# A graph-network kernel on four full engines: the adjacency is copied into the score bank by ScalarE, and the linear row is added by the instruction that takes the extreme

## The chip, the cores and the metric

The kernel runs on one core of a Trainium2 chip. The metric is the device time of one execution in microseconds: the kernel before takes 4812.59 us (median of three runs, 4811.78 to 4815.49).

## What is computed

The input `x` has 64 graphs of 256 nodes with 128 features; `adj` is one 256 x 256 adjacency for all. Everything is fp32. Four residual layers follow each other, each on `h = relu(layernorm(x))`:

- layer 0: five steps of a gated recurrence (`adj @ h`, two gates, a tanh candidate);
- layer 1: Chebyshev hops with `adj`, a linear map, relu;
- layer 2: `adj @ h + h`, a linear map, rows divided by their norm;
- layer 3: pairwise attention, in the reference

```python
pre = s1[:, :, None, :] + s2[:, None, :, :] + b_lin
h = jnp.where(pre >= 0, pre, ALPHA * pre)
e = jnp.einsum('bije,e->bij', h, a) + bias
attn = jax.nn.softmax(e, axis=2)
out = jax.nn.sigmoid(jnp.einsum('bij,bjf->bif', attn, x))
```

In the first line `s1` and `s2` are `h` times the two halves of `adj` (it stands in the place of `W`). For each of 64 graphs layer 3 needs 256 x 256 node pairs with 256 features each: this is where the time goes. In the end the 256 x 256 scores `e` of a graph are the sum of three things: a nonlinear part, for each pair of nodes and each feature; the adjacency; and a part linear in `s2`, one row of 256 numbers per graph ("the linear row"; what is linear in `s1` falls out of the softmax).

## The kernel before

**Tiles and scores.** The graphs go in 32 pairs. A pair's query nodes are cut into 64 slots of four nodes for each of both graphs (2048 slots in all; 32 slots are a *unit*, that is 128 query nodes of both graphs). A slot has two tiles `rl` of 128 x 4 x 2 x 256 numbers (features by query nodes by graphs by the other nodes), the minimum or the relu of what `s1` and `s2` give: kind 0 (first half of the features) and kind 1 (second half). `work_on_tile` (L933 on) makes them: VectorE kind 0 in one instruction (L953), ScalarE kind 1 in eight (L961), GpSimd either kind in eight (L967). TensorE's `score` sums a tile over its features with a window of signs and adds the result into the unit's bank of the accumulator memory (PSUM), in eight matmul instructions (L1041).

**Joined slots.** In a share of the slots, `SHARE = (4, 13)`, GpSimd makes the second tile in a form of its own (kind 2), and a transfer that GpSimd issues adds it to the slot's kind 0 tile in memory (`add_pair`, L987). Such a slot is scored once, not twice. The last 96 slots have none. There are 14 tile buffers.

**A unit's bank.** Each unit's scores accumulate in a bank of 128 x 512 (two graphs by 256). `bank_ready` (L997) and `fill_bank` (L1004) fill it before the first score: one VectorE instruction (L1006) writes adjacency rows plus the linear row `lin`. The first pair's two units ("alone": its graphs are treated one by one) instead get the adjacency by matmuls in `score`. `tail` (L827) follows the unit's last score. VectorE adds an odd feature's step (L839, two instructions of 128 x 256: minimum of `s2o` and `s1o`, plus the bank, into `sc`), takes the maximum of the rows, negated (L844); ScalarE takes exponentials with it as bias (L848); then come a turn on TensorE (L447), a copy (L856), the product with `h3`, and `o` (L876), which SyncE sends out. For the first two units the tail also adds `lin`.

**The other work.** `front` brings a pair through layers 0 to 2 and makes the operands of layer 3. Its steps are small instructions on all engines; `norm` (L475) goes from VectorE (statistics) over GpSimd (inverse roots) to ScalarE. `lin` and `s2o` come through small transfers by way of main memory into the tile `rows`.

**What sets the order.** The program is written out in one order per engine by a planner (the loop at the end of the function). `ran(engine, us, ...)` (L106) advances a clock of planned durations, such as `TURN`, `STATS`, `ELEMENTS`; whichever engine's clock is least takes the next thing that is ready. Tails come first, then fronts, then fills, added pairs or scores, then new tiles. So tiles are shared out by the planned durations, not on the chip: there each engine runs its list in order and waits on semaphores.

Of the kernel before, what the change touches and what calls it, by code (L numbers as in the profile page):

```python
# [8 lines left out]
F32 = mybir.dt.float32  # L9
AF = mybir.ActivationFunctionType  # L10
OP = mybir.AluOpType
AX = mybir.AxisListType
PSUM = bass.MemoryType.PSUM

P = 128
NB = 2
# [5 lines left out]
MOST_POSITIVE = -MOST_NEGATIVE  # L22
PE, DVE, ACT, POOL = ENGINES = (mybir.EngineType.PE, mybir.EngineType.DVE, mybir.EngineType.Activation, mybir.EngineType.Pool)
SLOTS = 64
SHARE = (4, 13)
AHEAD_OF = 2
ALONE = 96
LOW = 1
# [4 lines left out]
def kernel(  # L33
# [50 lines left out]
    nc = tc.nc  # L84
    B, N, D = x.shape
# [20 lines left out]
    def ran(engine, us, *after):  # L106
        start = max(clock[engine], 0.0, *after)
        clock[engine] = start + us
        return clock[engine] + SEEN[engine]
# [10 lines left out]
    def of_spare(bank):  # L120

        return [b for b in spare if bank < 2 or id(b[0]) in WRITTEN]
# [14 lines left out]
    def by_feature(b, nb=NB):  # L137
        return b[:, 0:nb * N].rearrange("p (b n) -> p b n", b=nb)
# [320 lines left out]
    def feat(name, **kw):  # L459
        return work.tile([P, NB, N], F32, name=name, **kw)  # L460
# [7 lines left out]
    SHORT = dict(tag="short", bufs=12)  # L468


    PROJECT, MIX, TURN, PRODUCT, PRODUCTS = (None, 0.44, 0.86), (None, 0.88, 1.74), (None, 0.38, 0.60), (None, 0.45, 0.88), (None, 1.33, 2.64)
    COPY, BIASED, TANH, ELEMENTS = (None, 0.32, 0.48), (None, 0.40, 0.58), (None, 0.40, 0.57), (None, 0.36, 0.61)
    NORMED, STATS, LAST = (None, 0.78, 1.55), (None, 0.50, 0.87), (None, 0.55, 1.04)

    def norm(src, since, h):  # L475

        nb = src.shape[1]
        stats = work.tile([P, nb * NC, 3], F32, name="stats", bufs=4)
        mv = work.tile([P, nb * NC, 2], F32, name="mv", bufs=4)
        s, h = rows_of(src), rows_of(h)[:, :, 0:D]  # L480
        yield DVE, since
        for k in range(0, nb * NC, 2):
            nc.vector.bn_stats(stats[:, k:k + 2, :].rearrange("p k s -> p (k s)"), s[:, k:k + 2, :].rearrange("p k d -> p d k"))
        nc.vector.tensor_reduce(mv[:, :, 0], stats[:, :, 1:2], AX.X, OP.add, negate=True)
        t = ran(DVE, STATS[nb], since) + 0.1
        yield POOL, t
        inverse_root(mv[:, :, 1], stats[:, :, 2], 1.0 / D, OP.mult, LN_EPS, OP.add)
        nc.gpsimd.tensor_mul(mv[:, :, 0], mv[:, :, 0], mv[:, :, 1])  # L488
        t = ran(POOL, 1.69, t)
        yield ACT, t  # L490
        for k in range(nb * NC):
            nc.scalar.activation(h[:, k, :], s[:, k, :], AF.Relu, bias=mv[:, k, 0:1], scale=mv[:, k, 1:2])  # L492
        return ran(ACT, NORMED[nb], t)

    READY = {}
# [327 lines left out]
    def across(u):  # L823

        return [(0, c) if READY[u]["alone"] else (c, u[1]) for c in range(NB)]

    def tail(u, pe, since):  # L827

        ops = READY[u]
        x3, h3, pe = ops["x3"], ops["h3"], [by_feature(pe[0])[:, k, :] for k in range(NB)]  # L830
        yield DVE, max(since, ops["t_lin"])
        used = banks_of.pop(u)[0]
        if ops["alone"]:
            nc.vector.tensor_add(by_feature(used), by_feature(used), ops["lin"].to_broadcast([P, NB, N]))
            since = ran(DVE, ELEMENTS[2], since, ops["t_lin"])
            yield DVE, since
        sc = feat("sc", **SHORT)
        for k, (b, c) in enumerate(across(u)):
            nc.vector.scalar_tensor_tensor(sc[:, k, :], ops["s2o"][:, b, :], ops["s1o"][:, b, c:c + 1], pe[k], op0=OP.min, op1=OP.add)  # L839
        t = ran(DVE, 0.8, since)  # L840
        spare.append([used, t])
        yield DVE, t
        nmx = work.tile([P, NB], F32, name="nmx")
        nc.vector.tensor_reduce(nmx, sc, AX.X, OP.max, negate=True)  # L844
        t = ran(DVE, ELEMENTS[2], t)
        yield ACT, t
        for b in range(NB):
            nc.scalar.activation(sc[:, b, :], sc[:, b, :], AF.Exp, bias=nmx[:, b:b + 1], scale=1.0)  # L848
        t_s = ran(ACT, 0.8, t)
        yield PE, t_s, 1  # L850
        b = take()
        to_token(b[0], sc)
        t = ran(PE, TURN[2], t_s, b[1])
        yield ACT, t
        wT = tok("wT", **SHORT)
        nc.scalar.copy(wT, by_token(b[0]))  # L856
        t = ran(ACT, COPY[2], t)
        spare.append([b[0], t])
        yield PE, t, 1
        bank = take()  # L860
        po = bank[0][:, :NB * (D + 1)].rearrange("p (b d) -> p b d", b=NB)
        for k, (b, _) in enumerate(across(u)):
            for c in range(NC):
                side_by_side(po[:, k, :], wT[:, k, c, :], h3[:, b, c, :], c == 0, c == NC - 1)
        t = ran(PE, PRODUCT[2], t, bank[1])
        yield DVE, t
        rs = work.tile([P, NB], F32, name="rs")
        nc.vector.reciprocal(rs, po[:, :, D])
        t = t_s = ran(DVE, 0.15, t)
        yield ACT, t  # L870
        for k in range(NB):
            nc.scalar.activation(po[:, k, 0:D], po[:, k, 0:D], AF.Tanh, scale=rs[:, k:k + 1])
        t = ran(ACT, 0.9, t, t_s)
        yield DVE, t
        o = work.tile([P, NB, D], F32, name="o")
        nc.vector.scalar_tensor_tensor(o, po[:, :, 0:D], 0.5, x3[:, 0] if ops["alone"] else x3[:, :, u[1], :], op0=OP.mult, op1=OP.add)  # L876
        t = ran(DVE, 0.36, t)
        spare.append([bank[0], t])
        p, k = u
        nc.sync.dma_start(out[p * NB + k].rearrange("(c p) d -> p c d", p=P) if ops["alone"] else  # L880
                          out[p * NB:(p + 1) * NB, k * P:(k + 1) * P, :].rearrange("b p d -> p b d"), o)
        TAILED.add(u)
# [8 lines left out]
    banks_of = {}  # L891
# [105 lines left out]
    def bank_ready():  # L997

        u = next((u for u in UNITS if u not in left and u not in banks_of), None)
        if u not in READY or READY[u]["alone"] or len(banks_of) == 2 or all(where(slot(k))[0] < u for k in range(3)):  # L1000
            return None
        return (max(READY[u]["t_lin"], min(b[1] for b in of_spare(2))), u) if of_spare(2) else None

    def fill_bank(u):  # L1004
        bank, free = take(2)
        nc.vector.tensor_add(by_feature(bank), adj_n[:, u[1]:u[1] + 1, :].to_broadcast([P, NB, N]), READY[u]["lin"])  # L1006
        banks_of[u] = bank, ran(DVE, ELEMENTS[2], free, READY[u]["t_lin"])

    def score_ready():

# [85 lines left out]
    while scored[0] < 2 * NSLOT or CHAINS:  # L1096
        while begun_fronts[0] < NPAIR and begun_fronts[0] < 2 + (scored[0] + 2 * SLOTS - 1) // (2 * SLOTS):
            begin_front()
        e = min(now, key=now.get)
        todo = []  # L1100
        for key in CHAINS:
            since = chain_ready(key, e)
            if since is not None:
                todo.append((since, (0, key) if isinstance(key, tuple) else (1, key), key))
        if e == PE:
            best = score_ready()
            if best:
                todo.append((best[0], (2,), best[1]))
        else:
            since = tile_ready(e)  # L1110
            if since is not None:
                todo.append((since, (3,), None))
            if e == DVE and bank_ready():
                todo.append((bank_ready()[0], (2,), bank_ready()[1]))
            pair = pair_ready()
            if e == POOL and pair and e not in begun:
                todo.append((pair[0] + SLACK, (2,), pair[1]))
        ready = [x for x in todo if x[0] <= now[e] + 0.05]
        if ready:
            if e == PE and len(tiles) <= LOW:  # L1120
                ready = [x for x in ready if x[1] == (2,)] or ready
            _, (rank, *_), what = min(ready, key=lambda x: x[1])
            if rank < 2:
                advance(what)
            elif e == PE:
                score(what)
            elif e == DVE and rank == 2:
                fill_bank(what)
            elif rank == 2:
                add_pair(what)  # L1130
            else:
                work_on_tile(e)
            in_order()
            now[e] = max(now[e], clock[e])
        else:
            later = [x[0] for x in todo] + [t for t in now.values() if t > now[e]]
            now[e] = min(later) if later else now[e] + 1.0
# [31 lines left out]
```

## Time and profile before

| | |
|---|---|
| runs: median (lowest to highest) | 4812.59 us (4811.78 to 4815.49) |
| the profiled execution: its time, its span | 4794.9 us, 4793.1 us |
| mean granted TensorE clock | 0.997 |
| accumulating transfers (`rl<-rl`) | 600 of 1 MB, 8.1 us from issue to landing |
| that queue's packets | 65.5% of 16 transfer engines' span |
| VectorE tiles (L953) | 1743 |
| ScalarE tile instructions (L961) | 10104 |
| GpSimd tile instructions (L967) | 6280 and 2440 |
| scoring matmuls (L1041) | 17864 and 10104 |

Busy time of an engine is the union of its instructions' records. In a group of instructions the mean is that of single records, which overlap at their ends, so a start-to-start distance can be shorter than the mean. "Idle before" says what an engine waited for. The chain that ended last is followed back from the last instruction, each step to what released it. Names: `bank` is a PSUM bank, `rl` a tile, `rows` the tile that holds `lin` and `s2o`; PE is TensorE, PEld its weight loads, DVE VectorE, ACT ScalarE, POOL GpSimd, SP SyncE.

### The profile page before, as it was taken

How to read it: one execution, taken by the hardware profiler on the slowest of the kernel's cores; microseconds unless marked ns; L12 is line 12 of the kernel's file. 1: busy time of each engine (PE TensorE's matmuls, PEld its weight loads, DVE VectorE, ACT ScalarE, POOL GpSimd, SP SyncE). 2: the span in 40 equal slices, each digit the busy share in tenths (PEclk: the TensorE clock that was granted, in tenths of full speed). 3: DMA queues.
4: the chain of work that ended last, by engine and by line, in shares of the span. 5: the costliest groups of instructions: out<-in, count | busy, mean ns of one | idle time of the engine just before them, and what ended most of it. 6: DMA issues, size and time to landing. Idle time of an engine off the chain costs nothing.

```text
span 4793.1 us, 132928 instructions
## 1 busy us (share of the span) xinstructions
PE 4718.4 (98%) x51591; PEld 1740.7 (36%) x51591; DVE 4647.5 (97%) x3502; ACT 4659.3 (97%) x12220; POOL 4619.2 (96%) x9823
## 2 busy tenths in 40 slices
PE   9999999999999999999999999999999999999999
PEld 4333333333333333333333333333333333333333
DVE  5999999999999999999999999999999999999998
ACT  5999999999999999999999999999999999999999
POOL 2999999999999999999999999999999999999998
PEclk9999999999999999999999999999999999999999
DMA  0777777777777777777777777777767776777730
GB/s 23 157 143 152 146 152 150 144 149 154 152 143 154 146 146 157 147 151 145 150 146 155 149 148 147 149 151 154 148 139 153 155 150 142 145 151 148 147 69 5
DMA packets 131523, 672.70 MB, mean 140 GB/s; under 512 B 14920, under 2 KB 50120, under 8 KB 54088
## 3 DMA queue, kind: packets, MB, share of 16 engines
q0 software_dynamic: 86400, 629.18, 65.5%
q1 hardware_dynamic: 43768, 35.01, 2.5%
q8 instruction: 403, 6.60, 0.5%
q14 instruction: 232, 1.90, 0.1%
q10 hardware_dynamic: 720, 0.00, 0.0%
HBM read 26.48 MB, written 8.52 MB: 7 GB/s over the span
## 4 chain that ended last, share of the span: by engine, by line
PE 47%; DVE 15%; POOL 11%; ACT 8%; DMA 4%; issue 4%; POOLq 0%; DVEq 0%; ACTq 0%
PE bank L1041 31%; PE bank L414 14%; DVE rl L953 11%; POOL rl L967 9%; ACT rl L961 6%; DMA rl<-rl 4%; PE bank L447 1%; POOL rl L987 1%; DVE bank L1006 1%; ACT h L492 1%; PE bank L439 0%; DVE bank L626 0%; POOL mv L409 0%; DVE hT L630 0%; DVE d L622 0%
## 5 line engine op out<-in xcount | busy, mean ns | idle before, releaser
L961 ACT ACTIVATE rl<-bank,s1b 128x256 f32<-128x256 f32 x10104 | 4072.5, 833 | 10.1 <-DMA rl<-rl 6.5
L953 DVE TENSOR_TENSOR rl<-s1a,bank 128x2048 f32<-128x2048 f32 x1743 | 3894.9, 2277 | 26.1 <-DMA rl<-rl 13.1
L967 POOL TENSOR_SCALAR rl<-s2n,s1b 128x256 f32<-128x256 f32 x6280 | 3033.4, 829 | 13.9 <-DMA rl<-rl 3.1
L1041 PE MATMUL bank<-rl,win_n 128*32 128x512 f32 x17864 | 2226.3, 594 | 19.9 <-DMA rl<-rl 13.4
L1041 PE MATMUL bank<-rl,win 128*32 128x512 f32 x10104 | 1349.9, 594 | 0.0
L967 POOL TENSOR_SCALAR rl<-s2c,s1a 128x256 f32<-128x256 f32 x2440 | 1190.6, 783 | 5.2 <-PE bank L1041 1.4
L1041 PEld LDWEIGHTS bank<-rl,win_n 128*32 128x32 f32 x17864 | 583.5, 110 | 1181.0 <-issue 964.9
L987 POOL DMA_DIRECT2D rl<-rl x600 | 651.7, 1105 | 9.4 <-issue 4.8
L1041 PEld LDWEIGHTS bank<-rl,win 128*32 128x32 f32 x10104 | 335.1, 110 | 675.6 <-issue 529.4
L414 PE MATMUL bank<-mT,wts 128*32 128x512 f32 x2480 | 325.6, 595 | 4.5 <-DVE rh L587 4.5
L414 PE MATMUL bank<-adj_t,h 128*32 128x256 f32 x4960 | 297.8, 380 | 5.1 <-ACT h L641 5.0
L414 PEld LDWEIGHTS bank<-adj_t,h 128*32 128x32 f32 x4960 | 157.7, 110 | 165.8 <-ACT h L641 40.8
L492 ACT ACTIVATE h<-x,mv 128x128 f32<-128x128 f32 x376 | 170.4, 654 | 22.7 <-POOL mv L488 22.4
L583 ACT ACTIVATE bank<-bank,gate_b 128x512 f32<-128x512 f32 (+1 forms) x165 | 158.3, 959 | 17.1 <-PE bank L414 15.3
L414 PE MATMUL bank<-mT,w 128*32 128x512 f32 x1240 | 163.2, 596 | 0.0
L414 PE MATMUL bank<-rh,u5t 128*32 128x512 f32 x1240 | 162.7, 595 | 0.0
L414 PE MATMUL bank<-hT,wts 128*32 128x512 f32 x1240 | 162.1, 593 | 0.0
L539 ACT COPY mT<-bank 128x512 f32<-128x512 f32 x155 | 145.3, 937 | 16.0 <-PE bank L414 15.9
L606 ACT ACTIVATE bank<-bank,gate_b 128x512 f32<-128x512 f32 (+1 forms) x165 | 153.7, 931 | 6.1 <-PE bank L414 5.8
L619 ACT ACTIVATE bank<-bank,gate_b 128x512 f32<-128x512 f32 x155 | 147.2, 950 | 5.3 <-PE bank L414 5.2
L414 PEld LDWEIGHTS bank<-mT,wts 128*32 128x32 f32 x2480 | 81.0, 110 | 191.8 <-issue 132.5
L409 POOL TENSOR_TENSOR mv<-mv,minus_half 128x4 f32<-128x4 f32 (+1 forms) x132 | 134.2, 1017 | 11.0
(207 smaller groups left out, 3252.7 us busy)
## 6 DMA issues: line engine op xcount, KB each, us to landing
rl<-rl POOLq DMA_DIRECT2D x600, 1024.0 KB, 8.1
rows<-row SPq DMA_DIRECT2D x31, 512.0 KB
xin<-in_x_dram SPq DMA_DIRECT2D x64, 128.0 KB
out_dram<-o SPq DMA_DIRECT2D x64, 128.0 KB
row<-quarter SPq DMA_DIRECT2D x62, 2.0 KB
rows<-row SPq DMA_DIRECT2D x2, 256.0 KB
w_raw<-in_L_gnn_w_w_dram SPq DMA_DIRECT2D x3, 128.0 KB
rl<-in_L_gnn_Theta_dram SPq DMA_DIRECT2D x1, 320.0 KB
```

Of the source, the lines that this page charges most:

```text
L409: nc.gpsimd.tensor_tensor(t, t, minus_half[:, 0:t.shape[1]], op=OP.pow)
L414: nc.tensor.matmul(o[g:g + 32], w[:, g:g + 32], t, start=start, stop=stop, skip_group_check=True)
L492: nc.scalar.activation(h[:, k, :], s[:, k, :], AF.Relu, bias=mv[:, k, 0:1], scale=mv[:, k, 1:2])
L539: nc.scalar.copy(c, seen(bank))
L583: nc.scalar.activation(seen(r), seen(pr), AF.Tanh, bias=br, scale=0.5)
L606: nc.scalar.activation(seen(pr), seen(pr), AF.Tanh, bias=bz, scale=0.5)
L619: nc.scalar.activation(seen(pv), seen(pv), AF.Tanh, bias=bh_n, scale=-1.0)
L953: nc.vector.tensor_tensor(t, rows.to_broadcast(whole), ops["s2a"].unsqueeze(1).to_broadcast(whole), op=OP.min)
L961: nc.scalar.activation(t[:, g, b, :], other(ops["s2b"], b), AF.Relu, bias=rows[:, g, b], scale=-1.0)
L967: nc.gpsimd.tensor_scalar(t[:, part, b, :], other(ops["s2n" if k else "s2c"], b), rows[:, part, b], MOST_NEGATIVE, op0=OP.min, op1=OP.max)
L987: nc.gpsimd.dma_start(out=t.rearrange("p g b n -> p (g b n)"), in_=z.rearrange("p g b n -> p (g b n)"), accum_op=OP.add)
L1041: nc.tensor.matmul(pe[g * 32:(g + 1) * 32, :], w[:, 31 - r:63 - r], flat(t[:, g]), start=False, stop=(left[u] == 0), skip_group_check=True)
```

## The change

The share of joined slots becomes (1, 3). The bank is filled by ScalarE, with the adjacency alone, and the fill no longer depends on `lin`. In the tail the odd feature's step comes first and writes the bank in place; then two `tensor_tensor_reduce` instructions add `lin`, multiply by -1, write `sc`, and give the row's minimum as an accumulated output, so that the reduction apart goes and the exponential gets scale -1. The first two units go the same way, without an add of their own. In the planner `TURN` rises by 0.1 and the time from statistics to GpSimd by 0.4.

```diff
-SHARE = (4, 13)
+SHARE = (1, 3)
...
-    PROJECT, MIX, TURN, PRODUCT, PRODUCTS = (None, 0.44, 0.86), (None, 0.88, 1.74), (None, 0.38, 0.60), (None, 0.45, 0.88), (None, 1.33, 2.64)
+    PROJECT, MIX, TURN, PRODUCT, PRODUCTS = (None, 0.44, 0.86), (None, 0.88, 1.74), (None, 0.48, 0.70), (None, 0.45, 0.88), (None, 1.33, 2.64)
...
-        t = ran(DVE, STATS[nb], since) + 0.1
+        t = ran(DVE, STATS[nb], since) + 0.5
...
-        used = banks_of.pop(u)[0]
-        if ops["alone"]:
-            nc.vector.tensor_add(by_feature(used), by_feature(used), ops["lin"].to_broadcast([P, NB, N]))
-            since = ran(DVE, ELEMENTS[2], since, ops["t_lin"])
-            yield DVE, since
+        used, lin = banks_of.pop(u)[0], ops["lin"]
+        for k, (b, c) in enumerate(across(u)):
+            nc.vector.scalar_tensor_tensor(pe[k], ops["s2o"][:, b, :], ops["s1o"][:, b, c:c + 1], pe[k], op0=OP.min, op1=OP.add)
+        t = ran(DVE, 0.9, since, ops["t_lin"])
+        yield DVE, t
         sc = feat("sc", **SHORT)
+        nmx = work.tile([P, NB], F32, name="nmx")
         for k, (b, c) in enumerate(across(u)):
-            nc.vector.scalar_tensor_tensor(sc[:, k, :], ops["s2o"][:, b, :], ops["s1o"][:, b, c:c + 1], pe[k], op0=OP.min, op1=OP.add)
-        t = ran(DVE, 0.8, since)
+            nc.vector.tensor_tensor_reduce(sc[:, k, :], pe[k], lin[:, b, :], scale=-1.0, scalar=MOST_POSITIVE,
+                                           op0=OP.add, op1=OP.min, accum_out=nmx[:, k:k + 1])
+        t = ran(DVE, 0.8, t)
         spare.append([used, t])
-        yield DVE, t
-        nmx = work.tile([P, NB], F32, name="nmx")
-        nc.vector.tensor_reduce(nmx, sc, AX.X, OP.max, negate=True)
-        t = ran(DVE, ELEMENTS[2], t)
         yield ACT, t
         for b in range(NB):
-            nc.scalar.activation(sc[:, b, :], sc[:, b, :], AF.Exp, bias=nmx[:, b:b + 1], scale=1.0)
+            nc.scalar.activation(sc[:, b, :], sc[:, b, :], AF.Exp, bias=nmx[:, b:b + 1], scale=-1.0)
...
-        return (max(READY[u]["t_lin"], min(b[1] for b in of_spare(2))), u) if of_spare(2) else None
+        return (min(b[1] for b in of_spare(2)), u) if of_spare(2) else None
...
-        nc.vector.tensor_add(by_feature(bank), adj_n[:, u[1]:u[1] + 1, :].to_broadcast([P, NB, N]), READY[u]["lin"])
-        banks_of[u] = bank, ran(DVE, ELEMENTS[2], free, READY[u]["t_lin"])
+        nc.scalar.copy(by_feature(bank), adj_n[:, u[1]:u[1] + 1, :].to_broadcast([P, NB, N]))
+        banks_of[u] = bank, ran(ACT, 0.51, free)
...
-            if e == DVE and bank_ready():
+            if e == ACT and bank_ready():
...
-            elif e == DVE and rank == 2:
+            elif e == ACT and rank == 2:
                 fill_bank(what)
```

## The prediction

> **What bounds the kernel now.** I read the page's busy shares first, then the chain that ended last, then the groups that the diff touches, then the timeline around single fills.
>
> The busy shares (engine, busy us, share of the span, instructions):
>
> ```profile
> PE 4718.4 (98%) x51591; PEld 1740.7 (36%) x51591; DVE 4647.5 (97%) x3502; ACT 4659.3 (97%) x12220; POOL 4619.2 (96%) x9823
> ```
>
> Four engines are full at once. VectorE, ScalarE and GpSimd make the 4096 tiles between them, TensorE scores them, and a third to a half of the makers' missing time lies in the first 100 us (VectorE is busy for 48 of them, ScalarE 46, GpSimd 11 by the windows). So no engine is *the* bound: work taken from one maker is worth only its share of all makers' speed, because the planner shares the tiles out anew. That share is a choice of mine, checked against the chain (shares of the span by line, whole execution):
>
> ```profile
> by line: PE bank L1041 31.1%; PE bank L414 14.1%; DVE rl L953 11.4%; POOL rl L967 8.9%; ACT rl L961 5.9%; DMA rl<-rl 4.5%; issue 3.6%; PE bank L447 1.5%; POOL rl L987 1.1%; DVE bank L1006 0.7%; ACT h L492 0.7%; PE bank L439 0.5%; DVE bank L
> ```
>
> It wanders over all of them. Two entries matter: "DMA rl<-rl", the accumulating transfers, 4.5% or 216 us; and L1006, the bank fill, 0.7% or 34 us, much for 62 instructions. Its group, with the neighbours that I use as prices (count, then busy us, mean ns of one):
>
> ```profile
> L953 DVE TENSOR_TENSOR rl<-s1a,bank 128x2048 f32<-128x2048 f32 x1743 | 3894.9, 2277 | 26.1 <-DMA rl<-rl 13.1 <-POOL rl L967 5.8 <-PE bank L1041 4.6
> L1006 DVE TENSOR_TENSOR bank<-adj_n,rows 128x512 f32<-128x512 f32 x62 | 85.7, 1382 | 0.0
> L839 DVE SCALAR_TENSOR_TENSOR sc<-rows,s1o,bank 128x256 f32<-128x256 f32 x128 | 55.4, 474 | 7.6 <-PE bank L1041 7.6
> L844 DVE TENSOR_REDUCE nmx<-sc 128x2 f32<-128x512 f32 x64 | 43.3, 676 | 0.0
> L876 DVE SCALAR_TENSOR_TENSOR o<-bank,x 128x256 f32<-128x256 f32 x64 | 26.9, 420 | 7.1 <-ACT bank L872 6.9
> L868 DVE RECIPROCAL rs<-bank 128x2 f32<-128x2 f32 x64 | 10.6, 165 | 13.8 <-PE bank L414 12.5 <-ACT rl L961 1.2
> ```
>
> A fill has 512 columns like L844, yet means 1382 ns against 676. One of the twelve over 1.9 us, with GpSimd beside it (start, duration):
>
> ```profile
> 4064.07 0.68 DVE L622 TENSOR_TENSOR d<-bank,hT 128x512 f32<-128x512 f32 x1
> 4064.67 4.92 DVE L1006 TENSOR_TENSOR bank<-adj_n,rows 128x512 f32<-128x512 f32 x1
> 4069.51 0.69 DVE L626 SCALAR_TENSOR_TENSOR bank<-bank,d 128x512 f32<-128x512 f32 x1
> ```
> ```profile
> 4062.30 8.40 POOL L967 TENSOR_SCALAR rl<-s2n,s1b 128x256 f32<-128x256 f32 x16
> ```
>
> The fill has no idle before it; it lasts 4.92 us while GpSimd runs its tile through, and the front step L626 stands behind it. GpSimd loses too: over the trace, its runs of 8 tile instructions beside a fill average 4.53 us (30 runs), the others 3.95 (456); runs of 16, 8.13 and 7.44. That is 0.6 to 0.7 us for a fill.
>
> **The price of a microsecond on each maker.** A tile costs VectorE 3894.9/1743 = 2.235 us, ScalarE 8 x 4072.5/10104 = 3.22, GpSimd 8 x (3033.4+1190.6)/8720 = 3.88. The rates 0.447, 0.310 and 0.258 make 1.016 tiles a us, so a us taken from VectorE is worth 0.44 us of the span, from ScalarE 0.31, from GpSimd 0.25. It holds while GpSimd can exchange tiles with both others: of its 1090 tiles 600 are joined ones, and with 650 some 440 stay free.
>
> **VectorE, removed.** 62 fills: start to start they average 1.32 us, 62 x 1.32 = 82. 64 reductions L844, start to start 0.60: 38. The two first units' adds: 1. Together 121 us.
>
> **VectorE, added.** 128 tensor_tensor_reduce of 128x256, one operand in PSUM, one in SBUF, with an accumulated output; the trace has none. The two L839 instructions stay, only written into the bank (L626 writes a bank and takes what L630 takes into SBUF). The nearest row for the main part is L876, the same operands without a per-partition scalar: 420 ns, where the next starts 0.34 after it. By the row alone, 128 x 0.34 = 44 us. [...] Net -121 + 58 = -63 us (ends -77 and -22), worth -28 (-34 to -10).
>
> Would the new instruction stall like the fill? [...] The trace agrees: L1006 (adj_n and rows both in SBUF) spreads from 677 to 5343 ns, L839 (rows in SBUF, the bank in PSUM) only from 462 to 481. The new pair is bank and row, like L839. [...]
>
> **ScalarE.** 62 copies of adjacency rows into a bank. The like row is L668, a broadcast copy into a bank of the same 128x512; the next starts 0.51 after it. 62 x 0.51 = 32 us, worth +10 (ends 0.47, as the other copies, and 0.55: +9 to +10). Behind a fill in ScalarE's queue stand tiles and front copies; L668 and L700 have no idle before them, so I add no wait. The fill no longer waits for the linear row's transfers. That saves nothing, L1006 having no idle; the row is now first needed at the tail, half a pair later. ACTIVATE stays, with another sign of scale.
>
> **GpSimd and the transfers.** JOINED has 1952 x 4/13 = 600 slots (the page has 600 adds) and will have 650. 50 more issues, each 0.63 us before the next instruction: 31 us. Without fills GpSimd gets 62 x 0.6 = 37 back. Net -6, worth -1 (without the relief +8). Tiles made stay 4096. Each add moves 1 MB: the queue's 65.5% of the transfer engines becomes 71%.
>
> **TensorE.** 50 scores fewer. A score is eight matmul instructions; the chain has 64 of them in 6.87 us, so 0.86 us a score, 43 us in all. I don't add this to the sum: the makers remain, and 43 is more than they give. The bank is held one VectorE step longer in the tail; of 8 banks that is 64 times some 2 us, which I put at nothing (at most +3).
>
> **Planned durations.** TURN +0.1 and the statistics' +0.5 change only the order. GpSimd waits 16.1 us for statistics outside the first long waits, worth at most -4; ScalarE waits 11.6 for turned banks, at most -4. Above: 320 turns planned 0.1 us longer leave TensorE 32 us which the plan thinks used; at its 31% of the chain, +10. I take 0.
>
> [...]
>
> **Sum.** -28 + 10 - 1 = **-19 us**. The profiled execution took 4794.9 (span 4793.1); the runs' median is 4812.6, 17.7 above it, and I carry the difference over: 4775 and **4793**.
>
> Check by the chain, line by line: L1006 -34; scoring 1491 x 50/3496 = -21; transfers 216 x 50/600 = +18; issues 53 x 50/600 = +4; VectorE's tail (+20, of which the chain holds L839's 13%) +3; ScalarE (7% of its tiles are on the chain) +2; GpSimd -4. That is -32. As another path takes over when one is cut, it is the larger end.
>
> **Rivals.** *The stalls did more than their length* (0.17): a 5 us stall delays the front step behind it and all four orders; the chain's -32 is had in full, 4781. For it: L1006's 34 us of chain. Against: three quarters of the fills take under 1 us.
>
> *Nothing comes of it* (0.20): the reduction costs 0.77 (-10 + 10 - 1 = -1) or the new plan's order loses what is saved; 4803 to 4822, about 4812. For it: no row has this instruction. It begins to slow the kernel above 0.77 us.
>
> *Adds land late* (0.23, the slower side): of the 19.9 us that the L1041 matmuls with win_n stand idle, 13.4 are waits for rl<-rl, and landing takes 8.1 us at the median, up to 15.2, while the queue's work is 0.655 x 4793/600 = 5.2. The plan reckons 6.6. Each of the 650 also keeps two of 14 tiles until it lands. If the chain's transfer part grows not by 18 but by 50 us (23%), the chain's gain is gone; at 65, some 4828. For it: the chain's 216 us. Against: waits of all engines for rl<-rl sum to about 82 us, many of them weight loads' that cost little.
>
> **How the numbers follow.** The forecast has 0.40, its own range 4785 to 4802. 0.2% of 4812.6 is 9.6 us, about what measuring this kernel can tell from no change. Faster 0.40 + 0.17 = 0.57, same 0.20, slower 0.23. The range goes from 4766 (the full chain with the reduction's low end) to 4832.
>
> **What the next profile would show.** Right: no VectorE instruction of 128x512 with two SBUF operands, none over 0.8 us but tiles; ACT copies x62 near 0.5 us apart; 128 reductions of 0.34 to 0.55 us start to start; 650 adds, 3446 scores; runs of 8 on GpSimd all near 3.95; VectorE more tiles than 1743, by about 20. Wrong: reductions above 0.77, or a "DMA rl<-rl" share of the chain far above 5% with larger waits of TensorE for it.

## The result, and the profile after

The kernel after takes 4799.74 us (median of nine runs, 4797.11 to 4801.11), the kernel before beside it 4812.59 (4810.66 to 4819.12). The ratio is 0.997, 95% interval 0.9961 to 0.9979: 12.9 us faster, where 19.5 were forecast. A second comparison gave 4777.13 against 4797.68, ratio 0.9957 (0.9944 to 0.9969), 20.6 us.

The two profiled executions must not be subtracted. That of before took 4794.9 us, less than any of its nine runs; that of after 4800.0, like its runs. By the profiles alone the change would be 5 us slower. The level moves from one comparison to the next: in the later ones the kernel before has medians of 4797.7 to 4801.6 us and single runs of 4791 to 4814, so that 4794.9 is an ordinary time there. So times below are compared within one comparison, as ratios, and profiles are read for counts, prices and waits. The levels that the expectations name are those of the first comparison.

The page's busy shares and the chain by line, of the kernel after:

```profile
PE 4693.5 (98%) x51191; PEld 1721.1 (36%) x51191; DVE 4609.8 (96%) x3643; ACT 4686.1 (98%) x12250; POOL 4630.9 (97%) x9801
```
```profile
by line: PE bank L1039 24.8%; POOL rl L965 18.1%; PE bank L414 14.4%; ACT rl L959 12.9%; DMA rl<-rl 8.8%; DVE rl L951 6.0%; issue 3.3%; POOL rl L985 2.4%; PE bank L447 1.3%; ACT h L492 1.2%; POOL mv L409 0.7%; ACT bank L619 0.4%; PE bank L4
```

VectorE is 38 us less busy, TensorE 25, ScalarE 27 more. VectorE's fill has left the chain, and the accumulating transfers have gone from 4.5% to 8.8% of it. A chain is that of one execution: in the profile of the second comparison, of this same kernel, TensorE's part is 52% and not 41%, the transfers' 9.0%:

```profile
by line: PE bank L1039 31.6%; PE bank L414 17.7%; POOL rl L965 12.2%; ACT rl L959 11.2%; DMA rl<-rl 9.0%; DVE rl L951 5.7%; issue 2.7%; PE bank L447 1.6%; POOL rl L985 1.6%; ACT h L492 0.9%; PE bank L439 0.5%; POOL mv L409 0.5%; ACT bank L6
```

So differences of ten points in TensorE's part say little. The groups that answer to those shown of before:

```profile
L951 DVE TENSOR_TENSOR rl<-s1a,bank 128x2048 f32<-128x2048 f32 x1756 | 3923.8, 2278 | 29.6 <-DMA rl<-rl 16.4 <-PE bank L1039 7.7 <-POOL rl L965 3.7
L834 DVE SCALAR_TENSOR_TENSOR bank<-rows,s1o,bank 128x256 f32<-128x256 f32 x128 | 62.4, 487 | 21.8 <-PE bank L1039 19.4
L840 DVE CUSTOM_DVE_ANT_0 sc<-bank,rows 128x256 f32<-128x256 f32 x128 | 48.6, 417 | 0.0
L840 DVE DVE_READ_ACCUMULATOR2_ANT nmx<- 128x1 f32 x128 | 10.6, 83 | 0.0
L1004 ACT COPY bank<-adj_n 128x512 f32<-128x512 f32 x62 | 63.1, 1018 | 0.0
L1039 PE MATMUL bank<-rl,win_n 128*32 128x512 f32 x17496 | 2197.0, 594 | 61.6 <-DMA rl<-rl 50.2 <-DVE rl L951 7.2 <-POOL rl L965 1.6
```

VectorE makes 13 tiles more (1756 for 1743). The fill costs ScalarE 0.52 us start to start (its 1018 ns overlap with its neighbours). The scores are (17496 + 10072)/8 = 3446. In the last row TensorE's matmuls now stand idle for 50.2 us behind adds (40.7 in the second profile); before it was 13.4:

```profile
L1041 PE MATMUL bank<-rl,win_n 128*32 128x512 f32 x17864 | 2226.3, 594 | 19.9 <-DMA rl<-rl 13.4
```

A tail's two new instructions on VectorE's timeline (start, duration):

```profile
197.40 0.41 DVE L840 CUSTOM_DVE_ANT_0 sc<-bank,rows 128x256 f32<-128x256 f32 x1
197.74 0.08 DVE L840 DVE_READ_ACCUMULATOR2_ANT nmx<- 128x1 f32 x1
197.74 0.42 DVE L840 CUSTOM_DVE_ANT_0 sc<-bank,rows 128x256 f32<-128x256 f32 x1
198.08 0.08 DVE L840 DVE_READ_ACCUMULATOR2_ANT nmx<- 128x1 f32 x1
198.08 2.28 DVE L951 TENSOR_TENSOR rl<-s1a,bank 128x2048 f32<-128x2048 f32 x1
```

Each is two instructions in this trace, 128 of either in the run, but the accumulator read (81 to 85 ns by its record) starts together with what follows it: 0.34 us from one to the next, the low end of the 0.34 to 0.55 that the prediction named.

### The profile page after: what moved, and what is told of

It reads as the page before. It is cut to its first block, busy times and chain, and to the rows that moved or that the text cites. A ratio compares the mean times of both kernels' runs of the same rounds, so it can differ in the third digit from the quotient of the medians.

```text
span 4798.0 us, 132133 instructions
## 1 busy us (share of the span) xinstructions
PE 4693.5 (98%) x51191; PEld 1721.1 (36%) x51191; DVE 4609.8 (96%) x3643; ACT 4686.1 (98%) x12250; POOL 4630.9 (97%) x9801
## 4 chain that ended last, share of the span: by engine, by line
PE 41%; POOL 22%; ACT 17%; DMA 9%; DVE 7%; issue 3%; POOLq 0%; ACTq 0%; DVEq 0%
PE bank L1039 25%; POOL rl L965 18%; PE bank L414 14%; ACT rl L959 13%; DMA rl<-rl 9%; DVE rl L951 6%; POOL rl L985 2%; PE bank L447 1%; ACT h L492 1%; POOL mv L409 1%; ACT bank L619 0%; PE bank L439 0%; ACT sc L846 0%; ACT bank L606 0%; ACT bank L583 0%
## 5 line engine op out<-in xcount | busy, mean ns | idle before, releaser
L965 POOL TENSOR_SCALAR rl<-s2n,s1b 128x256 f32<-128x256 f32 x6312 | 3112.3, 931 | 10.6 <-DMA rl<-rl 0.8
L1039 PE MATMUL bank<-rl,win_n 128*32 128x512 f32 x17496 | 2197.0, 594 | 61.6 <-DMA rl<-rl 50.2
L1039 PEld LDWEIGHTS bank<-rl,win_n 128*32 128x32 f32 x17496 | 562.8, 110 | 1222.3 <-issue 908.0
L985 POOL DMA_DIRECT2D rl<-rl x650 | 780.6, 1223 | 3.3 <-issue 1.1
```

What stands on the lines that cost most here:

```text
L965: nc.gpsimd.tensor_scalar(t[:, part, b, :], other(ops["s2n" if k else "s2c"], b), rows[:, part, b], MOST_NEGATIVE, op0=OP.min, op1=OP.max)
L985: nc.gpsimd.dma_start(out=t.rearrange("p g b n -> p (g b n)"), in_=z.rearrange("p g b n -> p (g b n)"), accum_op=OP.add)
L1039: nc.tensor.matmul(pe[g * 32:(g + 1) * 32, :], w[:, 31 - r:63 - r], flat(t[:, g]), start=False, stop=(left[u] == 0), skip_group_check=True)
```

## The experiments

The change has three parts: the *edit* (fill on ScalarE, new tail), the *share* of joined slots, and the two planned *durations*. The theory was the prediction's sum: prices per microsecond of a maker, TensorE with room. The rivals were late adds and stalls that do more than their length.

### The share undone in the kernel after

```diff
-SHARE = (1, 3)
+SHARE = (4, 13)
```

> The changed kernel with the old share of joined slots, 600 adds. My sum (a microsecond of each maker has its price, TensorE has room): 50 issues of 0.63 us at 0.25 come back, -8 us, so about 4792. Adds that land late take the gain: the chain's transfer share falls from 8.8% back to about 4.5%, GpSimd's runs of 8 tile instructions from 4.05 us to 3.95, and the time to 4775 to 4790. TensorE's relief is what pays: 43 us more of scores, at TensorE's half of the chain, 4815 to 4820.

4781.84 us against 4801.6 for before: ratio 0.9961 (0.9948 to 0.9973). The kernel after stands at 0.997 and 0.9957 in its two comparisons, so the share alone makes no difference here that these runs can tell. (4781.84 lies in the range that was named for late adds only because the level of this comparison is lower: the kernel before is some 11 us below its first median.) The waits moved as late adds say: the matmuls wait for adds 9.0 us, not 50.2:

```profile
L1039 PE MATMUL bank<-rl,win_n 128*32 128x512 f32 x18016 | 2226.1, 593 | 12.8 <-DMA rl<-rl 9.0 <-DVE rl L951 3.6
```

But the time did not follow, so something else in this kernel had taken the gain. The runs below look for it.

### The share alone in the kernel before

```diff
-SHARE = (4, 13)
+SHARE = (1, 3)
```

> The kernel before with the new share alone, 650 adds. My sum: +8 us, 4820. Late adds: 4830 to 4840, the chain's transfer share near 9%. TensorE's relief pays: 4785 to 4795, and then the rest of the change gave nothing.

4830.1 us, ratio 1.0059 (1.0047 to 1.0072): 28 us slower, where my sum had 8 and late adds 17 to 27 (4830 to 4840, over the 4812.6 of the first comparison). TensorE's 43 us of relief do not pay. The matmuls' group and the chain by line:

```profile
L1041 PE MATMUL bank<-rl,win_n 128*32 128x512 f32 x17408 | 2219.2, 595 | 73.5 <-DMA rl<-rl 54.6 <-DVE rl L953 17.5
```
```profile
by line: PE bank L1041 24.3%; DVE rl L953 14.2%; PE bank L414 13.5%; POOL rl L967 12.5%; ACT rl L961 9.4%; DMA rl<-rl 9.2%; issue 5.1%; POOL rl L987 1.7%; PE bank L447 1.3%; ACT h L492 0.8%; DVE bank L1006 0.6%; POOL mv L409 0.6%; DVE bank 
```

TensorE stands 54.6 us behind adds in place of 13.4, and the chain's transfer share is 9.2%. The median landing goes only from 8.1 to 8.6 us: it is not that each add takes much longer, but that more scores come to stand behind one (57 waits of these matmuls in place of 15). Not all of the 28 us need be adds: the fills too are longer in this profile, 106.9 us of busy time for 85.7.

```profile
L1006 DVE TENSOR_TENSOR bank<-adj_n,rows 128x512 f32<-128x512 f32 x62 | 106.9, 1723 | 0.0
```

### The durations undone in the kernel after

```diff
-    PROJECT, MIX, TURN, PRODUCT, PRODUCTS = (None, 0.44, 0.86), (None, 0.88, 1.74), (None, 0.48, 0.70), (None, 0.45, 0.88), (None, 1.33, 2.64)
+    PROJECT, MIX, TURN, PRODUCT, PRODUCTS = (None, 0.44, 0.86), (None, 0.88, 1.74), (None, 0.38, 0.60), (None, 0.45, 0.88), (None, 1.33, 2.64)
...
-        t = ran(DVE, STATS[nb], since) + 0.5
+        t = ran(DVE, STATS[nb], since) + 0.1
```

> The changed kernel with the old planned durations of the turn and of the statistics' way to GpSimd. My sum puts them at nothing: 4795 to 4805. If the new order lost what was saved, 4785 or less; if these two durations are what pays, 4810 or more.

4781.96 us, ratio 0.9963 (0.9949 to 0.9977), between the 0.9957 and 0.997 of the kernel after. With the new share the planned durations make no difference that shows: as the prediction had it, in sum.

### The edit alone

The kernel after with both undone:

```diff
-SHARE = (1, 3)
+SHARE = (4, 13)
...
-        t = ran(DVE, STATS[nb], since) + 0.5
+        t = ran(DVE, STATS[nb], since) + 0.1
```

and `TURN` as before (0.38, 0.60).

> The fill on ScalarE and the new tail alone; share and planned durations as before. My sum without the 50 adds: VectorE -28, ScalarE +10, GpSimd's relief 37 x 0.25 = -9, so 27 us below the kernel before (22 to 32). If adds are dearer than 0.63 us each, this is also 8 us or more below the changed kernel. If the fill's move gave nothing and the share did it, within 5 us of the kernel before.

4760.04 us against 4797.68: ratio 0.992 (0.9907 to 0.9934), 37.6 us faster, beyond the 22 to 32 that the sum allowed, and 17 us below the unaltered kernel after in the same comparison (4777.13; no run of the one reaches the other's). This version beats both kernels: the edit brings all of the gain, and share and durations together take about half of it away. Its chain by line:

```profile
by line: PE bank L1039 38.0%; PE bank L414 19.2%; ACT rl L959 12.7%; POOL rl L965 7.2%; DVE rl L951 6.4%; DMA rl<-rl 4.5%; issue 2.4%; PE bank L447 1.8%; ACT h L492 1.0%; POOL rl L985 0.8%; PE bank L439 0.7%; POOL mv L409 0.3%; ACT h L641 0
```

TensorE now holds 60% of it (47% before); a chain differs nearly that much between two executions of one kernel, so TensorE's own waits say more. In the kernel before, TensorE stands idle for 19.6 us before its turns of `hT`, a tile of the front, nearly all of it for L630, the VectorE step that writes `hT`:

```profile
L447 PE MATMUL bank<-ident,hT 128*128 128x128 f32 x620 | 103.0, 289 | 19.6 <-DVE hT L630 18.8 <-ACT rl L539 0.5
```

In the edit alone it is 3.5 us. The fill of 4.92 us that the prediction shows (from 4064.67) is one of four, of 4.4 to 5.3 us, behind which TensorE runs dry. Its matmul there, and two windows (busy time of PE, PEld, DVE, ACT and POOL, then granted clock, DMA share, GB/s):

```profile
4073.03 1.12 PE L447 MATMUL bank<-ident,hT 128*128 128x128 f32 x4 [3.70 <-DVE hT L630]
```
```profile
4064.67:4071.48 6.81, 4.67 (x44) 1.17 (x36) 6.81 (x4) 6.81 (x20) 6.02 (x13) 1.00 0.59 119
4071.48:4078.30 6.82, 5.26 (x24) 1.71 (x28) 6.82 (x5) 3.76 (x10) 5.39 (x12) 0.50 0.66 135
```

TensorE idles 3.70 us, and towards the end of the wait its granted clock falls to 0.50 for 6.8 us. The other three go the same way (two for `hT`, the last for `rh`, another step of the front): idle 4.4, 3.0 and 2.4 us, and half the clock for 6.8, 3.4 and 3.4 us around the end of the wait. In this profile no other stretch from 130 us to 60 us before the end has less than the full clock; the edit alone has none there at all. TensorE's waits behind the first 120 us sum to 57 us before and 33 in the edit alone. These 24 us, and some 10 us for the 20.5 us at half clock (an estimate: from 4074.08 sixteen score matmuls take 3.41 us start to start there, from 4064.86 at the full clock 1.72), are the 34 us by which the two profiled spans differ (4793.1 and 4759.3; the profile of before lies at the level of this comparison, whose runs of before go from 4795 to 4801). The clock of all runs of this comparison agrees: 0.996 to 0.997 for before, 0.998 to 0.999 for the edit alone. So the edit's gain was had on TensorE, the engine that was said to have room. That an idle TensorE is what lowers its clock was not tested: a wait of 2.4 us at 4587 us, behind an add, has no such stretch after it.

The unaltered kernel ran beside it as a mark:

> The changed kernel, unaltered, as a mark beside the others on one chip: 13 us below the kernel before, as measured already.

It is the second comparison of the section above: 20.6 us, not 13.

### The fill without a stall, but on VectorE

From the edit alone:

```diff
-        nc.scalar.copy(by_feature(bank), adj_n[:, u[1]:u[1] + 1, :].to_broadcast([P, NB, N]))
-        banks_of[u] = bank, ran(ACT, 0.51, free)
+        nc.vector.tensor_copy(by_feature(bank), adj_n[:, u[1]:u[1] + 1, :].to_broadcast([P, NB, N]))
+        banks_of[u] = bank, ran(DVE, ELEMENTS[2], free)
...
```

(the lines left out give the fill to VectorE in the planner's loop)

> As edit_alone, but VectorE copies the adjacency into the bank: one SBUF operand instead of two, so the stall goes while the fill stays on VectorE. If the stall beside GpSimd is what the fill cost, all 62 last under 0.8 us, GpSimd's runs of 8 stay at 3.9, and the time lies near edit_alone: VectorE +62 x 0.60 x 0.44 = +16, ScalarE -10, so 6 us above it. If it is VectorE's time as such that counts, or a copy from SBUF stalls as well, it loses most of the gain, 15 us or more above edit_alone.

4762.74 us, ratio 0.9926 (0.9914 to 0.9938): 2.7 us above the edit alone. All fills of this run (count, then shortest, median and longest in ns):

```profile
L1004 DVE COPY bank<-adj_n x62: 678/684/694, 239.4 to 4629.3; 128x512 f32<-128x512 f32 x62
```

Before they ran from 677 to 5343. With one SBUF operand none of the 62 stalls. So which engine does the fill matters little here (2.7 us); the long fills came with the second SBUF operand. (This fill also no longer depends on `lin`; L1006 had no idle before it that this could save. The new tail with the old fill was not run.) By the sum, this run should gain less than it did: the stalls were 82 - 62 x 0.60 = 45 us of VectorE, the tail costs it 15 more (two times 0.47 + 0.34 in place of two times 0.39 and 0.60), and GpSimd gets back about 28 (62 x 0.45, from the last experiment): -45 x 0.44 + 15 x 0.44 - 28 x 0.25 = -20. Measured: -35. The stalls did more than their length, as the first rival said, here by some 15 us: TensorE stands idle for 0.8 us before its turns of `hT` in this run, and it too has the full clock from 130 us to 60 us before the end.

### The reduction apart

From the edit alone:

```diff
-        for k, (b, c) in enumerate(across(u)):
-            nc.vector.tensor_tensor_reduce(sc[:, k, :], pe[k], lin[:, b, :], scale=-1.0, scalar=MOST_POSITIVE,
-                                           op0=OP.add, op1=OP.min, accum_out=nmx[:, k:k + 1])
+        nc.vector.tensor_add(sc, by_feature(used), lin.to_broadcast([P, NB, N]) if ops["alone"] else lin)
...
+        nc.vector.tensor_reduce(nmx, sc, AX.X, OP.max, negate=True)
...
```

(the exponential has scale 1 again)

> As edit_alone (0.992 of the kernel before), but the linear row is added by one instruction of 128x512 and the extreme taken by a reduction of 128x512. By the rows: two of 0.60 us start to start in the place of two of 0.35, +0.51 us for each of 64 units, 33 us of VectorE, worth 14 us: ratio about 0.995. If VectorE's time no longer counts beside TensorE, which has most of the chain in edit_alone, within 5 us of it: 0.992 to 0.993.

4765.65 us against 4801.64, ratio 0.9923 (0.9908 to 0.9938), against 0.992: 33 us more of VectorE's time for no difference that the intervals can tell. The 0.992 is from another comparison; in the same one stands the run with the statistics planned longer, two sections on, 4763.59 us, which is 2.1 us less. The instruction that adds the row and takes the extreme at once is cheap and buys nothing here. The price of 0.44 us is not a constant: these 33 us hardly reach TensorE, whose waits behind the first 120 us sum to 34.5 us here and 32.8 in the edit alone.

### Fewer joined slots

From the edit alone:

```diff
-SHARE = (4, 13)
+SHARE = (2, 7)
```

> As edit_alone with still fewer joined slots: 2 in 7, 557 adds, so 43 scores more (37 us of TensorE) and 43 adds less. If an add costs GpSimd some 1.2 us with what it slows, 43 x 1.2 x 0.25 = 13 us are saved on the makers, but TensorE is near full: I expect it within 8 us of edit_alone, and above it if TensorE is the bound by now (then +15 to +20).

4776.85 us, ratio 0.9955 (0.9941 to 0.9968): 16.8 us above the edit alone for 43 scores (37 us of TensorE) more. The makers' saving is not seen. TensorE has 67% of the chain, which fits it as the bound:

```profile
by line: PE bank L1039 42.7%; PE bank L414 21.6%; DVE rl L951 9.4%; POOL rl L965 6.4%; ACT rl L959 4.3%; DMA rl<-rl 4.2%; issue 2.7%; PE bank L447 2.1%; PE bank L439 0.8%; POOL rl L985 0.6%; ACT h L492 0.4%; DVE bank L626 0.3%; DVE d L622 0
```

So the share has a cost on both sides of 600 adds: TensorE's scores below it, late adds above it (0.9963 with 650, from the run with the old durations, where the matmuls wait for adds 42.0 us and not 12.0):

```profile
L1039 PE MATMUL bank<-rl,win_n 128*32 128x512 f32 x17472 | 2207.8, 595 | 52.7 <-DMA rl<-rl 42.0 <-DVE rl L951 9.7 <-POOL rl L965 0.3
```

### The two durations, one by one

Each from the edit alone; the first changes `TURN` from (None, 0.38, 0.60) to (None, 0.48, 0.70), the second the statistics' step:

```diff
-        t = ran(DVE, STATS[nb], since) + 0.1
+        t = ran(DVE, STATS[nb], since) + 0.5
```

> As edit_alone with the turn planned 0.1 us longer, nothing else. The two planned durations together cost 0.4% at the old share (0.9961 against 0.992). The turn is the cause if TensorE, whose time the plan then overrates by 32 us, is left with less to do than it could: ratio 0.995 to 0.997. If it is the statistics' way, this one stays at 0.992 to 0.993.

> As edit_alone with the statistics' way to GpSimd planned 0.4 us longer, nothing else. My prediction took this and the turn at nothing. If it is the cause: 0.995 to 0.997, else 0.992 to 0.993.

4778.12 us, ratio 0.995 (0.9936 to 0.9963), for the turn; 4763.59, 0.9919 (0.9906 to 0.9933), for the statistics, both in one comparison. The turn costs 14.5 us beside the statistics, which cost nothing that shows. The turn's matmuls, in the edit alone and with the turn planned longer:

```profile
L447 PE MATMUL bank<-ident,hT 128*128 128x128 f32 x620 | 101.5, 286 | 3.5 <-DVE hT L630 3.0 <-ACT rl L539 0.5
```
```profile
L447 PE MATMUL bank<-ident,hT 128*128 128x128 f32 x620 | 102.3, 288 | 17.3 <-DVE hT L630 15.5 <-ACT hT L539 1.4
```

TensorE's idle time before these turns rises from 3.5 to 17.3 us, nearly all of it waiting for `hT`; with its other waits it goes from 33 to 55 us. These waits are of the size of the loss; which step of the new order makes them was not traced. This also answers the first experiment: going back to 600 adds there brings nothing, because at that share the longer turn costs about as much (0.992 becomes 0.9961 with both durations). With the new share, where TensorE has 43 us less to do, it costs nothing visible. That TensorE's greater room is the reason fits, but was not shown apart.

### Do adds slow GpSimd's tiles?

Two kernels look at GpSimd alone. The first has no joined slots:

```diff
-SHARE = (4, 13)
+SHARE = (0, 13)
```

> The kernel before without joined slots: no accumulating transfers, every tile scored by itself (600 more scores, some 515 us of TensorE, so 5150 to 5350 us, TensorE-bound). It is run for GpSimd's tile instructions. If transfers or the writing of their descriptors slow these beyond the 0.63 us of an issue, a run of 8 falls from 3.95 us beside no fill to about 3.63, as in the last 190 us of the kernel before; if not, it stays at 3.9.

In the second, SyncE issues plain copies between two tile buffers set aside for it, at the slots that were joined; twelve tile buffers remain:

```diff
...
-    JOINED = [n for n in range(NSLOT - ALONE) if (n + 1) * SHARE[0] // SHARE[1] > n * SHARE[0] // SHARE[1]]
+    COPIED = {n for n in range(NSLOT - ALONE) if (n + 1) * SHARE[0] // SHARE[1] > n * SHARE[0] // SHARE[1]}
+    JOINED = []
...
             following[k] += 1
+            if k == 0 and begun[e][0] in COPIED:
+                nc.sync.dma_start(out=idle_out, in_=idle_in)
```

> The kernel before without joined slots, but SyncE's queue issues 600 plain copies of 1 MB from one buffer in SBUF to another, at the slots that were joined; no transfer is issued by GpSimd. GpSimd's run of 8 tile instructions took 3.63 us without transfers and 3.95 with GpSimd's own. If it is the traffic in SBUF that slows GpSimd, it rises to 3.8 or more here; if it is GpSimd's own work for a transfer it issued, it stays at 3.65 or less.

They took 5211.63 and 5365.35 us (one run each), and runs of 8 averaged 3.63 and 3.62 us (the copies were not held back by anything and were all done by 2900 us; the second figure is of that stretch). Taken as I had set it up, this says that an add slows the tiles after it by 0.3 us. It does not. GpSimd's timeline without adds and, in the kernel after, with them:

```profile
1999.57 3.63 POOL L967 TENSOR_SCALAR rl<-s2n,s1b 128x256 f32<-128x256 f32 x8
2003.41 3.61 POOL L967 TENSOR_SCALAR rl<-s2n,s1b 128x256 f32<-128x256 f32 x8 [0.22 <-PE bank L1041]
```
```profile
2003.71 8.24 POOL L965 TENSOR_SCALAR rl<-s2n,s1b 128x256 f32<-128x256 f32 x16
2010.89 1.90 POOL L985 DMA_DIRECT2D rl<-rl  x1
2011.51 8.36 POOL L965 TENSOR_SCALAR rl<-s2n,s1b 128x256 f32<-128x256 f32 x16
```

The run of 16 is 8.24 us by its record, but the next instruction starts after 7.18: 3.59 for eight. Without adds it is 3.62 (3.84 less 0.22 of idle). The last record of a run is longer when adds are about; the pace is not slower. Start to start, runs of 8 with no fill beside them average 3.62 and 3.64 us behind an issue and 3.56 and 3.59 behind anything else, in the kernels before and after. An add costs GpSimd its 0.63 us and about 0.05. The reading by record length, in the prediction too, was wrong as a measure; for the tiles beside a fill, the same start-to-start count gives a median of about 0.45 us lost, not 0.6. The kernel without adds shows one thing more: three of its 62 fills, which still have two SBUF operands, find GpSimd idle throughout and last 690 ns, and the six longest, 2.6 to 3.4 us, have its tile instructions beside them throughout. So the stall needs no adds, and it was not seen where GpSimd stood still.

## Why the prediction was right, and where its terms were not

**The sign and the size** hold: 12.9 and 20.6 us for a forecast of 19.5. That they hold so well is luck: they are the difference of two terms that were both too small, 27 for the edit where it gave 38, and 8 for the share where it cost 20 or more. One of the signs that the prediction named for being wrong came as well, a transfer share far above 5% of the chain with larger waits of TensorE (8.8%, and 50.2 us for 13.4); the edit's surplus covered it. The level, 4793, came out as 4799.7 in one comparison and 4777.1 in the other.

**The edit** was put at -28 + 10 - 9 = -27 us and gave -38. Its prices were near. The fills are gone (82 us of VectorE); the reduction cost 0.34 us in place of 0.45 (44 us, not 58); what I put at nothing, the odd feature's step in place, takes 0.47 start to start where it took 0.39, 10 us. Net -67 us for -63. ScalarE's 62 x 0.52 = 32 is as said. GpSimd's relief is 28 us, not 37. What failed is the step from prices to time: "worth 0.44". For the stalls it was too low: the four of 4.4 us and more hold up a front step behind them, TensorE runs dry and then has half its clock, as the section on the edit alone shows. The first rival (0.17) names the delay, not the clock. For VectorE's evenly spread work it was too high: 33 us of it, in the reduction apart, could not be seen.

**Operands and the accumulated output.** That a fill with two SBUF operands is the one that stalls carried the forecast; L1006's spread (677 to 5343 ns) stood for it, and the fill on VectorE with one agrees: 678 to 694 ns for all 62. The new instruction, bank and row like L839, does not stall either: 412 to 424 ns for all 128 in the kernel after. The 58 us that the sum takes for these 128, 0.45 each, no run shows, nor the 0.77 of the other end: both were my estimates, above L876's 0.34. The kernel after shows 0.34 with the accumulated output in it, 44 us, so the term was 14 us of VectorE too high.

**The share** was put at +8 us (50 issues of 0.63 at 0.25) and costs 20 (0.992 to 0.9963) to 28 us (before, alone). The mis-sized step is that the main sum gave the longer queue of transfers no price; the check by the chain had one, +18, but took -21 for fewer scores beside it. This is the rival of the slower side: its mechanism came, with matmuls idle 40 to 50 us behind adds, and took half of the edit's gain, but not the whole. What spoke against it there, that many of these waits are weight loads' and cost little, can't be leant on: the weight loads of the scores wait for adds 103 us in the kernel after with the old durations and 51 in the edit alone, and TensorE's scores take 110.9 ns a matmul there, start to start without idle, and 109.8 here, 30 us in all.

**TensorE has room** was the wrong picture. With the edit in, 37 us more of scores cost 17. Before it too TensorE was busy for 98% of the span, with 57 us of waits behind the first 120 us, and the edit paid by what it took from these waits and from half-clock time. A maker's microsecond counted where it kept TensorE waiting; a general price for it missed that.

**The planned durations** at nothing: right for the kernel as changed, by chance of the share; with the old share the turn costs 14.5 us, beyond the +10 that I gave as its end.

**Carrying over 17.7 us** from the profiled execution to the runs had no ground in the kernel, as the levels of the later comparisons show; it did no harm to the difference.

## What to carry to other kernels

Try a VectorE instruction beside a busy GpSimd with one SBUF operand: with two, 12 of 62 fills took over 1.9 us here (up to 5.34), with one none took over 0.694. Such a stall cost more than its length where TensorE ran dry behind it (idle for 2.4 to 4.4 us, then 3.4 or 6.8 us at a granted clock of 0.50): look at the other engines' waits and at the granted clock. Where several engines are full, a price per microsecond holds only near the point where it was taken: test a balance parameter on both sides again after every edit, since the best of the three shares tried here was still the old one. Take an engine's pace from start to start: GpSimd's tile instructions had a median record of 794 ns with adds in the kernel after and 480 without, and the same pace, 3.59 and 3.62 us for eight.

## What the runs showed of the hardware that was not expected

The accumulator read has a median record of 83 ns, yet the following instruction starts with it (both at 197.74 in the timeline of the kernel after). A scalar_tensor_tensor of 128x256 that writes its bank in place takes 0.47 us start to start against 0.39 into SBUF: 0.52 to the second of its pair, 0.40 from the second to what follows. Two other instructions (L626 and L630, 128x512) take 0.60 either way; why is open. With adds in flight the median record of GpSimd's 128x256 tile instructions (`s2n,s1b`) is 724 ns in the kernel before and 794 in the kernel after, against 480 without adds, at the same pace. The granted clock falls to 0.50 for 3.4 or 6.8 us at a stroke: in the kernel before four times in mid-run, each time at a TensorE wait of 2.4 to 4.4 us behind a stalled fill, and in the kernel after three times, at waits of 2.6 to 3.0 us for adds.
